# Four state groups of one channel half in a row, with B spread once per step, in the selective scan of a four-layer network

## The chip, the cores and the metric

The kernel runs on one core of a Trainium2 chip. The metric is the device time of one execution in microseconds (us). Seventeen runs of the kernel before have a median of 8440.55 us (8407.6 to 8468.6).

The engines are named as in the profile: PE (matrix products; PEld is its weight load), DVE (vector), ACT (activation), POOL (a second elementwise engine), SP (here it only issues DMAs).

## What is computed

The reference has four layers on a 4 x 96 x 64 x 64 tensor. Only layer 0 is touched. It runs two "mamba" blocks over each image, seen as a sequence of 4096 positions with 96 channels. A block, cut to what matters:

```python
xz = h @ in_w                                  # h: layer norm of seq
xs, z = jnp.split(xz, 2, axis=-1)              # 192 channels each
xc = silu(conv4(xs) + conv_b)                  # 4 taps along the sequence
dbl = xc @ xproj_w                             # dt (6), B (16), C (16)
delta = softplus(dt @ dt_w + dt_b)
dA = exp(delta[..., None] * A)                 # 192 channels x 16 states
dBx = delta[..., None] * Bm[:, :, None, :] * xc[..., None]
hstates = associative_scan(dA, dBx)            # h[t] = dA[t] h[t-1] + dBx[t]
y = einsum('bldn,bln->bld', hstates, Cm) + Dp * xc
seq = seq + (y * silu(z)) @ out_w
```

After the second block come a small product (`fus_w`) and a batch norm.

## The kernel before, in words

**Tiling.** A *unit* is one chunk of 512 positions of one image (4), one block i (2) and one chunk index (8): 64 units, in that order. The 192 channels are two halves of 96, the 16 states four groups nq of 4. One *step* handles one group of one half: 96 x 4 = 384 rows, held as three tiles of 128 partitions (32 channels x 4 states each). A unit has eight steps, numbered m = 0 to 7 here; a table `ORDER` says which group and half each is. The code calls a step v (over all units) and divides it into four quarters q = 0 to 3.

**A step.**
- `states_in` (L564): PE spreads the group's four rows of B from the tile `dbl` over 128 partitions, into the one PSUM bank `Bb`.
- `inputs` (L571, DVE): `bt = xR * Bb`, all three tiles at once. `xR` is delta*x of the half, each channel repeated for the 4 states.
- `decay` (L582, ACT): `a_ps = exp(A * dR)`, one of the three tiles, in one of three banks. `dR` is delta, repeated like `xR`.
- `states` (L598, DVE): the scan of one tile, three a step. It reads `a_ps` and writes `bt` in place.
- `outputs`: ACT copies the last column to `carry` (L606), then POOL multiplies `bt` by the broadcast rows of C (`Cb`, L607).
- `collect` (L621, L624, PE), two steps later: sums the 4 states of each channel into the bank `yp`; the first step of a half also adds `Dp * xc` (L621).

**Around the steps.** `output` (L635, ACT) copies a finished `yp`. `finish` is called in parts: POOL's `xc * sz` (L640); then PE's L644 (the residual) and L646 (the output product); then ACT's L648; and for i = 1 also PE's L654, then ACT's L656 with DVE's L657. `replicate` is six DMAs that make the `dR` and `xR` of a half from a DRAM tile `spread`.

**Preparation.** `prepare` computes all that a unit needs before its steps. It is a generator with 34 or 35 pieces between its yields. Counted from 0, those that matter here are: 0 L420, 3 L429 and the halo copy L434, 6 L440 (DVE), 7 L442, 8 and 9 the conv L450 (four matmuls a half, sixteen records in all), 11 and 12 L457, 13 to 15 the gate L460, L462, L464 on ACT and then POOL's L465, 18 L471 (`dbl`'s product), 20 L475 (its copy) with the DMA of the C rows, 21 L481, 23 and 24 L488/L489, 25 L491, 26 L494, 27 L497 (DVE), 28 L503 with POOL's L504 and PE's L507, 29 POOL's L509, 30 L516 with POOL's L517, 31 to 33 the second gate L522, L524, L527 and POOL's L528.

**What sets the order.** The schedule is manual: each engine gets its instructions in the order in which the loop at L676 to L708 emits them. At quarter 4m + q of unit u it first calls the pieces of the next units that are due. With PERIOD 32, piece k of unit u+1 is due at quarter k - AHEAD of unit u (negative: in the unit before). Then, in this order and each at its own quarter: a part of `finish`, `states_in` of the next step (q = 1), `output`, `collect` of the step two back (q = 3), the scan and the decay two ahead (q = 0, 1, 2), and at q = 3 `outputs` of this step and `inputs` of the next.

With AHEAD 14, the conv falls in step 6, L471 in step 1, L504 and L509 in step 3, L517 and L528 in step 4. L640 is issued at step 2, q = 2, and L644 with L646 at step 4, q = 1.

B is spread five times a unit: where two neighbouring steps have the same group, they use the same `Bb`.

**Buffers before.** `bt` four tiles, `Cb` six, `dR` and `xR` three each; PSUM banks: two `mm` (all of `prepare`'s and `finish`'s products), three `a_ps`, one `Bb`, two `yp`.

Of the kernel before, what the change touches and what calls it, by code (L numbers as in the profile page):

```python
# [10 lines left out]
F32 = mybir.dt.float32  # L11
# [4 lines left out]
PSUM = bass.MemoryType.PSUM  # L16
DRAM = bass.MemoryType.DRAM

B, C, H, W = 4, 96, 64, 64
# [320 lines left out]
def layer0(k, X):  # L340

    tc, nc, ins = k.tc, k.nc, k.ins
    T = NB
    NCH = L // T
    NQ, NG, PS = 4, 3, 4
    NT = 2 * NQ
    ORDER = ((0, 0), (0, 1), (1, 0), (1, 1), (2, 0), (3, 0), (3, 1), (2, 1))
    LAST = {hf: max(m for m, o in enumerate(ORDER) if o[1] == hf) for hf in range(2)}
    with ExitStack() as es:

        nc.scalar.preload_act_table_set("natural_log_exp_and_others")
# [9 lines left out]
        seln = k.load(wp, "c_seln", (128, NQ, 128))  # L361
# [24 lines left out]
        def pool(name, bufs, **kw):  # L386
            return scan.enter_context(tc.tile_pool(name=f"l0{name}", bufs=bufs, **kw))

        p1, p2, p3 = pool("p1", 1), pool("p2", 2), pool("p3", 3)
        bp, cp = pool("b", 4), pool("c", 6)  # L390
        dram = pool("dram", 3, space=DRAM)
        pm, pa = pool("pm", 2, space=PSUM), pool("pa", 3, space=PSUM)
        pb, py = pool("pb", 1, space=PSUM), pool("py", 2, space=PSUM)
        fbs = {}

        def mm():
# [19 lines left out]
        def prepare(b, i, ch, st, before):  # L416
# [25 lines left out]
            nc.scalar.activation(h[:, 3:], d, AF.Identity, bias=k.v(f"ln_b{i}"))  # L442
            yield

            xc = st["xc"] = p3.tile([C, 2, T], F32, name="xc")
            ps = []
            for hf in range(2):
                p = mm()
# [4 lines left out]
                ps.append(p)  # L453
                yield
            yield
            for hf, p in enumerate(ps):
                nc.scalar.activation(xc[:, hf], p[:C], AF.Identity, bias=k.v(f"conv_b{i}{hf}"))  # L457
                yield
# [17 lines left out]
            out = dram.tile([16, T], F32, name="out_states")  # L476
            nc.sync.dma_start(out, dbl[64:80])
            yield
            ps = [mm() for _ in range(2)]
# [42 lines left out]
            nc.scalar.activation(gate, sz, AF.Exp, scale=-1.0)  # L522
            yield
            nc.scalar.activation(gate, gate, AF.Ln, bias=k.one[:C])  # L524
            replicate(st, 0)
            yield
            nc.scalar.activation(gate, gate, AF.Exp, scale=-1.0)  # L527
            nc.gpsimd.tensor_mul(sz, sz, gate)  # L528
            yield
            st["Cb"] = [cp.tile([128, T], F32, name="Cb") for _ in range(NQ)]  # L530
            for nq, t in enumerate(st["Cb"]):
                nc.sync.dma_start(
                    t, out[PS * nq : PS * nq + PS].unsqueeze(0).to_broadcast([32, PS, T])
                )
            yield

        def replicate(st, hf):

            for n, name in enumerate(("dR", "xR")):
                t = st[name, hf] = p3.tile([128, NG, T], F32, name=name)  # L540
                for q in range(NG):
                    r = 96 * hf + 32 * q
                    nc.sync.dma_start(
                        t[:, q], st["spread"][n, r : r + 32].unsqueeze(1).to_broadcast([32, PS, T])
                    )

        units = [(b, i, ch) for b in range(B) for i in range(2) for ch in range(NCH)]
        V = NT * len(units)
        sts = [{} for _ in units]
        carries, bts, Bbs, dec, skips = {}, {}, {}, {}, {}  # L550

        def at(v):

            u, m = divmod(v, NT)
            return (sts[u], units[u], *ORDER[m])

        def states_in(v):

            st, _, nq, _ = at(v)
            if v and v % NT and ORDER[v % NT - 1][0] == nq:  # L560
                Bbs[v] = Bbs[v - 1]
                return
            Bb = Bbs[v] = pb.tile([128, T], F32, name="Bb")
            nc.tensor.matmul(Bb, seln[:, nq], st["dbl"], start=True, stop=True)  # L564

        def inputs(v):

            st, _, nq, hf = at(v)
            bt = bts[v] = bp.tile([128, NG, T], F32, name="bt")
            Bb = Bbs[v]  # L570
            nc.vector.tensor_mul(  # L571
                bt, st["xR", hf], Bb.unsqueeze(1).to_broadcast([128, NG, T])
            )

        def decay(n):

            v, q = divmod(n, NG)
            if v >= V:
                return
            st, (b, i, ch), nq, hf = at(v)  # L580
            dec[n] = pa.tile([128, T], F32, name="a_ps")
            nc.scalar.activation(  # L582
                dec[n], st["dR", hf][:, q], AF.Exp, scale=A[:, i, nq, hf, q : q + 1]
            )
# [17 lines left out]
        def outputs(v):  # L602

            st, _, nq, hf = at(v)
            bt = bts[v]
            nc.scalar.copy(carry_of(v), bt[:, :, T - 1])  # L606
            nc.gpsimd.tensor_mul(  # L607
                bt, bt, st["Cb"][nq].unsqueeze(1).to_broadcast([128, NG, T])
            )

        def collect(v):

            st, (b, i, ch), nq, hf = at(v)
            if nq == 0:
                yp = st["yp", hf] = py.tile([C, T], F32, name="yp")
                if ch == 0:
                    skips[hf] = p1.tile([C, C], F32, name=f"skip{hf}")
                    nc.vector.tensor_scalar(
                        skips[hf], k.ident[:C, :C], k.v(f"Dp{i}{hf}"), None, ALU.mult
                    )  # L620
                nc.tensor.matmul(yp, skips[hf], st["xc"][:, hf], start=True, stop=False)  # L621
            bt = bts.pop(v)
            for q in range(NG):
                nc.tensor.matmul(  # L624
                    st["yp", hf][32 * q : 32 * q + 32],
                    red,
                    bt[:, q],
                    start=False,
                    stop=v % NT == LAST[hf],
                )  # L630

        def output(u, hf):

            st, (b, i, ch) = sts[u], units[u]
            nc.scalar.copy(st["xc"][:, hf], st["yp", hf])  # L635
# [21 lines left out]
            nc.vector.bn_stats(stats[:, b, ch], xs)  # L657
            yield

        PERIOD, AHEAD = 4 * NT, 14  # L660

        with tc.manual_schedule():
            for _ in pooled(0):
                pass
            for _ in prepare(*units[0], sts[0], None):
                pass
            replicate(sts[0], 1)
            states_in(0)
            inputs(0)
            for n in range(2):  # L670
                decay(n)
            preps = [
                prepare(*units[u], sts[u], sts[u - 1]) if u else iter(()) for u in range(len(units))
            ]
            taken, task = [0] * len(units), iter(())
            for v in range(V + 7):  # L676
                u, m = divmod(v, NT)
                for q in range(4):
                    for w in range(u + 1, min(u + 3, len(units))):
                        while taken[w] <= 4 * v + q - PERIOD * (w - 1) + AHEAD:  # L680
# [12 lines left out]
                    if q == 2 and m == 2 and 0 < u <= len(units):  # L693
                        task = finish(u - 1)
                        next(task)
                    if q == 3 and 0 <= v - 2 < V:
                        collect(v - 2)
                    if v >= V:
                        continue
                    if q < NG:  # L700
                        states(NG * v + q)
                        decay(NG * v + q + 2)
                    if q == 3:
                        outputs(v)
# [1493 lines left out]
```

## Time and profile before

| | us |
|---|---|
| median of 17 runs | 8440.55 |
| the profiled execution | 8448.68 |
| its span, first to last instruction | 8446.9 |
| layer 0's steps: first L571, last L571 | 105.80, 3454.15 |

Busy in the stretch from 105 to 3460 (3355.0 us), with the granted clock of PE as a share of full speed:

| PE | PEld | DVE | ACT | POOL | PE clock |
|---|---|---|---|---|---|
| 2557.61 | 826.10 | 2873.04 | 2265.52 | 2637.20 | 0.83 |

How to read the lines that follow. A line of the timeline has the start, the duration, the engine, the line of the code, the operation, output <- inputs, the shapes and the number of instructions merged into the line; in brackets stands how long the engine had been idle and whom it waited for by the trace. "issue" there means a wait that the profile could not put down to anyone. A line of the groups has the count, then total busy us and the mean ns of one, then the engine's idle time just before. A line of the waits has the total us, how often, and the longest. An f32 matmul of the code shows as two records.

### The profile page before, as it was taken

The numbers are of one execution on the slowest core, as the hardware profiler recorded it, in microseconds if no ns is written. First come the engines' busy times: TensorE is split into PE (matmuls) and PEld (weight loads), VectorE is DVE, ScalarE is ACT, GpSimd is POOL, SyncE is SP. The second block draws the span as 40 slices with busy tenths as digits, with TensorE's granted clock in tenths as the row PEclk, the third lists the DMA queues.
The fourth block names the chain that finished last, engine by engine and source line by source line (L and its number), as shares of the span: only waits on it lengthen the run. The fifth ranks groups of instructions, "written<-read, shape, count | busy, mean of one in ns | idle before, by whom it ended". The sixth has DMA issues, their size and how long they took to land.

```text
span 8446.9 us, 76871 instructions
## 1 busy us (share of the span) xinstructions
PE 5981.6 (71%) x24218; PEld 2790.4 (33%) x24218; DVE 5719.6 (68%) x8127; ACT 3946.3 (47%) x7624; POOL 4696.2 (56%) x2915
## 2 busy tenths in 40 slices
PE   4777777777777777656688989897765656556553
PEld 1222222222222222422255555555442323333221
DVE  4888888888888888578865554545445555556555
ACT  4666666666666666333345555555521111111101
POOL 4877777778777877334444342424005555545553
PEclk8888888888888888777878888888877777767676
DMA  3322222222222222423210101010025444344443
GB/s 104 105 96 95 93 98 95 95 96 95 95 95 96 95 96 95 146 75 90 75 47 4 36 4 35 6 34 14 16 55 145 114 123 138 109 134 117 114 115 122
DMA packets 424413, 720.32 MB, mean 85 GB/s; under 512 B 188149, under 2 KB 190253, under 8 KB 419762
## 3 DMA queue, kind: packets, MB, share of 16 engines
q1 hardware_dynamic: 348710, 480.74, 18.4%
q0 software_dynamic: 73968, 227.47, 9.5%
q10 hardware_dynamic: 1328, 7.20, 0.2%
q8 instruction: 193, 3.16, 0.2%
q14 instruction: 214, 1.75, 0.1%
HBM read 567.04 MB, written 97.82 MB: 79 GB/s over the span
## 4 chain that ended last, share of the span: by engine, by line
PE 31%; DVE 18%; another core or an unknown queue 8%; ACT 7%; issue 7%; DMA 2%; POOL 2%; SPq 1%; DVEq 0%; ACTq 0%; POOLq 0%
PE sc_ps L1069 2%; DVE bt L598 2%; PE mm_ps L450 2%; PE pT_ps L1118 2%; DVE bt L571 2%; PE o_ps L1138 2%; DVE prod L2010 1%; PE yb_ps L1916 1%; DVE sm L2011 1%; PE yd_ps L2043 1%; PE Bb L564 1%; PE sT_ps L2031 1%; PE mm_ps L471 1%; PE m_ps L1527 1%
## 5 line engine op out<-in xcount | busy, mean ns | idle before, releaser
L607 POOL TENSOR_TENSOR bt<-bt,Cb 128x1536 f32<-128x1536 f32 x512 | 1763.4, 3444 | 678.2 <-issue 451.2
L598 DVE TENSOR_TENSOR_SCAN bt<-a_ps,carry,bt 128x512 f32<-128x512 f32 x1536 | 1865.1, 1265 | 58.2 <-ACT a_ps L582 11.0
L1993 POOL DMA_INDIRECT sm<-table,ix x1152 | 1097.2, 952 | 1300.4 <-DVE om L1970 494.7
L582 ACT ACTIVATE a_ps<-dR,w_l_A_log 128x512 f32<-128x512 f32 x1536 | 1053.2, 687 | 343.4 <-DVE bt L598 339.2
L571 DVE TENSOR_TENSOR bt<-xR,Bb 128x1536 f32<-128x1536 f32 x512 | 889.2, 1737 | 399.2 <-issue 189.8
L2031 PE MATMUL sT_ps<-ident,sd 128*128 128x128 f32 (+1 forms) x896 | 226.8, 376 | 716.8 <-ACT sT L2032 447.3
L564 PE MATMUL Bb<-dbl,w_c_seln 128*128 128x512 f32 x640 | 449.8, 792 | 380.1 <-DVE bt L571 380.1
L1106 POOL TENSOR_TENSOR p<-p,rs 128x392 f32<-128x392 f32 x384 | 312.0, 840 | 477.3 <-DVE rs L1104 417.1
L450 PE MATMUL mm_ps<-h,Wk 96*128 96x512 f32 x1024 | 567.3, 717 | 11.1 <-issue 6.8
L624 PE MATMUL yp<-bt,w_c_red 128*32 128x512 f32 x3072 | 560.3, 635 | 6.0 <-POOL bt L607 6.0
L471 PE MATMUL mm_ps<-xc,w_l_xp 96*128 96x512 f32 x256 | 235.6, 1076 | 290.9 <-POOL xc L465 290.9
L2031 PEld LDWEIGHTS sT_ps<-ident,sd 128*128 128x128 f32 (+1 forms) x896 | 133.9, 182 | 795.1 <-ACT sT L2032 474.3
L319 PE MATMUL bc_ps<-xs,w_l_bc 96*128 96x512 f32 x384 | 241.8, 763 | 215.3 <-DVE q L913 215.3
L1093 ACT ACTIVATE p<-p,rs 128x196 f32<-128x196 f32 x768 | 342.7, 449 | 82.6 <-DVE rs L1083 82.4
L2032 ACT COPY sT<-sT_ps 128x512 f32<-128x512 f32 (+1 forms) x256 | 122.0, 477 | 523.6 <-PE sT_ps L2031 266.4
L450 PEld LDWEIGHTS mm_ps<-h,Wk 96*128 96x128 f32 x1024 | 241.0, 238 | 365.2 <-issue 332.6
L2048 DVE SCALAR_TENSOR_TENSOR z<-yd_ps,vec,yb 96x512 f32<-96x512 f32 x32 | 23.9, 747 | 498.5 <-remote 286.5
L564 PEld LDWEIGHTS Bb<-dbl,w_c_seln 128*128 128x128 f32 x640 | 137.3, 242 | 652.2 <-DVE bt L571 493.2
L1929 ACT ACTIVATE go<-go_ps,w_l_go_b 18x512 f32<-18x512 f32 x32 | 21.7, 678 | 703.4 <-remote 524.3
L1916 PE MATMUL yb_ps<-X,w_l_base_w 96*128 96x504 f32 (+3 forms) x576 | 309.5, 702 | 0.3 <-ACT go L1930 0.3
L1126 DVE COPY pT<-pT_ps 98x512 f32<-98x512 f32 x256 | 176.0, 687 | 153.1 <-PE pT_ps L1118 145.6
L507 PE MATMUL mm_ps<-h,w_l_z_w 96*128 96x512 f32 x256 | 222.1, 1017 | 77.9 <-ACT w L503 77.9
(372 smaller groups left out, 13150.9 us busy)
## 6 DMA issues: line engine op xcount, KB each, us to landing
dR<-spread SPq DMA_DIRECT2D x384, 256.0 KB
xR<-spread SPq DMA_DIRECT2D x384, 256.0 KB
Cb<-out_states SPq DMA_DIRECT2D x256, 256.0 KB
spread<-w SPq DMA_DIRECT2D x128, 192.0 KB
spread<-dx SPq DMA_DIRECT2D x128, 192.0 KB
table<-xT SPq DMA_DIRECT2D x256, 96.0 KB
own<-vd SPq DMA_DIRECT2D x512, 36.8 KB
toep<-l_toep SPq DMA_DIRECT2D x12, 1536.0 KB
```

The source lines that it names most:

```text
L450: nc.tensor.matmul(p, Wk[:, i, t, hf], h[:, t : t + T], start=t == 0, stop=t == 3)
L471: nc.tensor.matmul(p, xp[:, i, hf], xc[:, hf], start=hf == 0, stop=hf == 1)
L564: nc.tensor.matmul(Bb, seln[:, nq], st["dbl"], start=True, stop=True)
L571: nc.vector.tensor_mul(bt, st["xR", hf], Bb.unsqueeze(1).to_broadcast([128, NG, T]))
L582: nc.scalar.activation(dec[n], st["dR", hf][:, q], AF.Exp, scale=A[:, i, nq, hf, q : q + 1])
L598: nc.vector.tensor_tensor_scan(t, dec.pop(n), t, carry_of(v)[:, q : q + 1], ALU.mult, ALU.add)
L607: nc.gpsimd.tensor_mul(bt, bt, st["Cb"][nq].unsqueeze(1).to_broadcast([128, NG, T]))
L624: nc.tensor.matmul(st["yp", hf][32 * q : 32 * q + 32], red, bt[:, q], start=False, stop=v % NT == LAST[hf],)
L1093: nc.scalar.activation(ps[n][:, h, i], ps[n][:, h, i], AF.Exp, scale=-1.0, bias=rs[n][:, 0, h, i : i + 1], accum_out=rs[n][:, 1, h, i : i ...
L1916: nc.tensor.matmul(dv[:, r0:r1, c0:c1], w_[:, t], av[b][:ch, 8 * n + r0 + dy : 8 * n + r1 + dy, c0 + dx : c1 + dx], start=t == 4, stop=t == 8,
L1993: nc.gpsimd.indirect_dma_start(sm[u][:, t].rearrange("p q c -> p (q c)"), None, samples[m // NN % 2], bass.IndirectOffsetOnAxis(ap=ix[m][: ...
L2031: nc.tensor.transpose(p[: e - 128 * q, q - q0], sf[:, 128 * q : e], k.ident)
```

## The change

1. The order of a unit's steps becomes: groups 0 to 3 of half 0 (steps 0 to 3), then groups 0 to 3 of half 1 (steps 4 to 7). The tables `ORDER` and `LAST` go.
2. `states_in` spreads B in every step, eight times a unit; no `Bb` serves two steps.
3. Buffers: `bt` six tiles, `dR` and `xR` two each; three `mm` banks, one `yp` bank.
4. AHEAD is 24 instead of 14, so every piece of `prepare` is emitted ten quarters earlier. The `xc` tile is taken after the conv's products instead of before them.
5. The replicating DMAs leave `prepare`: half 0 of the next unit is issued at step 3, q = 1, half 1 at step 7, q = 1. The broadcasts of C become a function, two groups each at steps 6 and 7, q = 3.
6. `output` is called at step 6 for half 0 and at step 2 of the next unit for half 1 (before: steps 1 and 2 of the next unit). The parts of `finish` after the first are called at (3,1), (3,3), (4,1), (4,3) instead of (4,1), (5,0), (5,1), (5,3).

```diff
-    ORDER = ((0, 0), (0, 1), (1, 0), (1, 1), (2, 0), (3, 0), (3, 1), (2, 1))
-    LAST = {hf: max(m for m, o in enumerate(ORDER) if o[1] == hf) for hf in range(2)}
...
-        bp, cp = pool("b", 4), pool("c", 6)
+        bp, cp = pool("b", 6), pool("c", 6)
...
-        pm, pa = pool("pm", 2, space=PSUM), pool("pa", 3, space=PSUM)
-        pb, py = pool("pb", 1, space=PSUM), pool("py", 2, space=PSUM)
+        pm, pa = pool("pm", 3, space=PSUM), pool("pa", 3, space=PSUM)
+        pb, py = pool("pb", 1, space=PSUM), pool("py", 1, space=PSUM)
...
             nc.scalar.activation(gate, gate, AF.Ln, bias=k.one[:C])
-            replicate(st, 0)
             yield
             nc.scalar.activation(gate, gate, AF.Exp, scale=-1.0)
             nc.gpsimd.tensor_mul(sz, sz, gate)
             yield
-            st["Cb"] = [cp.tile([128, T], F32, name="Cb") for _ in range(NQ)]
-            for nq, t in enumerate(st["Cb"]):
-                nc.sync.dma_start(
-                    t, out[PS * nq : PS * nq + PS].unsqueeze(0).to_broadcast([32, PS, T])
-                )
-            yield
...
-                t = st[name, hf] = p3.tile([128, NG, T], F32, name=name)
+                t = st[name, hf] = p2.tile([128, NG, T], F32, name=name)
...
+        def broadcast(st, nq):
+
+            t = st["Cb", nq] = cp.tile([128, T], F32, name="Cb")
+            src = st["out"][PS * nq : PS * nq + PS]
+            nc.sync.dma_start(t, src.unsqueeze(0).to_broadcast([32, PS, T]))
...
-            return (sts[u], units[u], *ORDER[m])
+            return (sts[u], units[u], m % NQ, m // NQ)
...
-            if v and v % NT and ORDER[v % NT - 1][0] == nq:
-                Bbs[v] = Bbs[v - 1]
-                return
-            Bb = Bbs[v] = pb.tile([128, T], F32, name="Bb")
-            nc.tensor.matmul(Bb, seln[:, nq], st["dbl"], start=True, stop=True)
+            Bbs[v] = pb.tile([128, T], F32, name="Bb")
+            nc.tensor.matmul(Bbs[v], seln[:, nq], st["dbl"], start=True, stop=True)
...
-        PERIOD, AHEAD = 4 * NT, 14
+        PERIOD, AHEAD = 4 * NT, 24
...
-            replicate(sts[0], 1)
+            for hf in range(2):
+                replicate(sts[0], hf)
+            for nq in range(NQ):
+                broadcast(sts[0], nq)
...
-                    if (m, q) in ((4, 1), (5, 0), (5, 1), (5, 3)):
+                    if (m, q) in ((3, 1), (3, 3), (4, 1), (4, 3)):
                         next(task, None)
...
+                    if q == 1 and m == 6 and u < len(units):
+                        output(u, 0)
+                    if q == 1 and m == 2 and 0 < u <= len(units):
+                        output(u - 1, 1)
+                    if u + 1 < len(units):
+                        if q == 1 and m in (3, 7):
+                            replicate(sts[u + 1], m // NQ)
+                        if q == 3 and m in (6, 7):
+                            for nq in (2 * m - 12, 2 * m - 11):
+                                broadcast(sts[u + 1], nq)
                     if q == 1 and v + 1 < V:
                         states_in(v + 1)
-                    if q == 1 and m in (1, 2) and 0 < u <= len(units):
-                        output(u - 1, m - 1)
...
-                        if m == LAST[0] and u + 1 < len(units):
-                            replicate(sts[u + 1], 1)
```

More of the change, by code (lines that the diff above doesn't have):

```diff
@@ L443, in prepare @@
             yield
-            xc = st["xc"] = p3.tile([C, 2, T], F32, name="xc")
             ps = []
@@ L455, in prepare @@
             yield
+            xc = st["xc"] = p3.tile([C, 2, T], F32, name="xc")
             for hf, p in enumerate(ps):
@@ L475, in prepare @@
             nc.scalar.copy(dbl, p)
-            out = dram.tile([16, T], F32, name="out_states")
+            out = st["out"] = dram.tile([16, T], F32, name="out_states")
             nc.sync.dma_start(out, dbl[64:80])
@@ L569, in inputs @@
             bt = bts[v] = bp.tile([128, NG, T], F32, name="bt")
-            Bb = Bbs[v]
+            Bb = Bbs.pop(v)
             nc.vector.tensor_mul(
@@ L607, in outputs @@
             nc.gpsimd.tensor_mul(
-                bt, bt, st["Cb"][nq].unsqueeze(1).to_broadcast([128, NG, T])
+                bt, bt, st["Cb", nq].unsqueeze(1).to_broadcast([128, NG, T])
             )
@@ L628, in collect @@
                     start=False,
-                    stop=v % NT == LAST[hf],
+                    stop=nq == NQ - 1,
                 )
```

## The prediction

> **How to count.** A unit is one 512-column chunk; its eight steps s0..s7 have four quarters q0..q3. Piece k of `prepare` (the code between two yields, from 0) runs at quarter k minus AHEAD of the unit before its own. All times are us.
>
> **What bounds it now.** I read the busy shares first, then the groups of the layer-0 stretch, the waits of that stretch, and then one unit in order of time. Layer 0's step loop runs from the first L571 at 105.80 to the last at 3454.15: 511 steps, 6.553 each, 52.42 a unit. The groups and the waits:
>
> ```profile
> L607 POOL TENSOR_TENSOR bt<-bt,Cb 128x1536 f32<-128x1536 f32 x512 | 1763.4, 3444 | 678.2 <-issue 451.2
> L598 DVE TENSOR_TENSOR_SCAN bt<-a_ps,carry,bt 128x512 f32<-128x512 f32 x1536 | 1865.1, 1265 | 58.2 <-ACT a_ps L582 11.0
> L571 DVE TENSOR_TENSOR bt<-xR,Bb 128x1536 f32<-128x1536 f32 x512 | 889.2, 1737 | 399.2 <-issue 189.8
> ```
> ```profile
> DVE bt L571 <- issue: 189.8, 59, 4.4
> DVE bt L571 <- PE Bb L564: 188.7, 97, 4.0
> ```
>
> DVE does the scans and sets the pace: a step without a wait takes 5.41 (L571 at 2009.47 and 2014.88). Eight steps, with 1.17 for the L497 pair and 0.44 for L440, make 44.9. The unit shown next (i = 0) took 51.51, so some 6.6 is waiting, all before L571, at two places:
>
> ```profile
> 2031.63 1.12 PE L644 MATMUL mm_ps<-X,ident 96*128 96x512 f32 x2
> ...
> 2032.60 1.88 PE L646 MATMUL mm_ps<-xc,w_l_out_w 96*128 96x512 f32 x4
> ...
> 2034.31 1.02 PE L564 MATMUL Bb<-dbl,w_c_seln 128*128 128x512 f32 x2
> ...
> 2035.44 1.75 DVE L571 TENSOR_TENSOR bt<-xR,Bb 128x1536 f32<-128x1536 f32 x1 [3.11 <-PE Bb L564]
> ...
> 2044.50 8.93 PE L450 MATMUL mm_ps<-h,Wk 96*128 96x512 f32 x16
> ...
> 2053.36 1.06 PE L624 MATMUL yp<-bt,w_c_red 128*32 128x512 f32 x6
> ...
> 2054.34 1.13 PE L564 MATMUL Bb<-dbl,w_c_seln 128*128 128x512 f32 x2
> ...
> 2055.57 1.75 DVE L571 TENSOR_TENSOR bt<-xR,Bb 128x1536 f32<-128x1536 f32 x1 [3.40 <-issue]
> ```
>
> Both times L571 starts 0.1 after L564 ended. L564 (the B spread) is short, but PE's matmuls run in code order, and it stands behind the output product L646 (s4) or behind the conv L450 (s6). The second wait, which the page puts down to "issue", is thus also for Bb and not for a bt buffer.
>
> **What costs nothing.** Six bt tiles: no wait for a bt buffer is seen above. Three more B spreads a unit: 0.86 of PE each (L564 2034.31 to L420 2035.17); each may start when L571 has freed the one Bb bank (1.75 into a step) and needs 1.0 to 2.1, so it ends 1.5 before DVE wants it, unless something stands ahead of it; that is priced below. With the cover gone it costs its own 1.0 to 2.1. Two replication tiles: the half-0 DMAs are issued at s3q1, after the last reads of that half, and read first from s7q1, four steps (21.6) later; six issues took 4.0 here and the first xR was used 6.2 after its issue. Half 1 and the C broadcasts have at least one step more than that queue needs; SP's waits hold no other engine's work. One yp bank: the copy L635 is two quarters ahead of the L621 that needs the bank. Three mm banks: each bank's reader (L503, L516, L425, L440, L648) stands quarters before the next writer. If an ACT copy were late there, PE would lose its 0.6.
>
> **What the earlier preparation does.** AHEAD 24 moves every piece by ten quarters against the scan. On POOL, L504 (piece 28), L509 and L517 fall in s1q0..q2, L528 in s2q1, and L640 stays at s2q2. POOL's order from s0 on becomes L607(s0), L504, L509, L517, L607(s1), L528, L640. `finish`'s second part (L644, L646) moves from s4q1 to s3q1, where it stands on PE ahead of the B spread for s4. So that spread now waits for L640; behind it on PE stand a collect and the conv. DVE waits for the spread, ACT's L457 for the conv. POOL's starts in this trace:
>
> ```profile
> 1028.30 3.44 POOL L607 TENSOR_TENSOR bt<-bt,Cb 128x1536 f32<-128x1536 f32 x1 [0.86 <-POOL xc L640]
> 1031.69 2.36 POOL L504 TENSOR_TENSOR dx<-dx,e 96x1024 f32<-96x1024 f32 x1
> 1034.12 2.35 POOL L509 TENSOR_TENSOR w<-w,dx 96x1024 f32<-96x1024 f32 x1
> 1036.43 3.45 POOL L607 TENSOR_TENSOR bt<-bt,Cb 128x1536 f32<-128x1536 f32 x1
> 1039.85 2.35 POOL L517 TENSOR_TENSOR dx<-w,xc 96x1024 f32<-96x1024 f32 x1
> 1042.16 2.37 POOL L528 TENSOR_TENSOR sz<-sz,gate 96x1024 f32<-96x1024 f32 x1
> 1044.50 3.42 POOL L607 TENSOR_TENSOR bt<-bt,Cb 128x1536 f32<-128x1536 f32 x1
> ```
>
> From one start to the next: 3.4 for L607, 2.43 for L504, 2.3 for the others. Two L607, L504 and four others make 18.6 from L607(s0)'s start to L640's end. Let 0 be the end of s0's scans. DVE wants s4's B spread at 18.0 (L497 1.17, three steps, L440 0.6). The sum of a unit with i = 0:
>
> - L607(s0) starts at 1.15: ACT must first copy the carry, and in s0 it now also has L488/L489, L491 and L494. Nearest row: 2021.70, 1.33 after the scans ended, with the same pieces about; without them 0.3. I count ACT's work through s0 (5.85 against DVE's 5.41) and get 1.15.
> - L640 ends at 19.75.
> - L646 and the B spread then take 2.73 with PE at speed (2032.60 to 2035.33) or 4.53 after a long pause. The pause: L644 has what it needs by about 14.5 and is done by 15.6, an estimate from the rows of L429, L621 and L624, so 4.2. The nearest row is L471, which paused 4.42; it and the spread behind it took 4.53 (2010.24 to 2014.77). I take 4.53. s4's L571 starts at 24.4, a wait of 6.4.
>
> ```profile
> 2010.24 3.30 PE L471 MATMUL mm_ps<-xc,w_l_xp 96*128 96x512 f32 x4 [4.42 <-POOL xc L465]
> ...
> 2013.33 1.44 PE L564 MATMUL Bb<-dbl,w_c_seln 128*128 128x512 f32 x2
> ...
> 2024.70 3.78 PE L507 MATMUL mm_ps<-h,w_l_z_w 96*128 96x512 f32 x4 [1.50 <-ACT w L503]
> ```
>
> - The conv (pieces 8 and 9) falls in s4q0 and s4q1, ahead of the spread for s5: collect 0.86, sixteen passes of 0.43 (1.71 for L646's four) or 6.9 at speed, 8.86 as in the unit shown (2044.50 to 2053.36); right behind other work I take 7.0. With the spread's 1.02 and the hand-over, s5's L571 starts 8.83 after the spread of s4 ended, where DVE wants it after 5.5: a second wait of 3.3.
> - Three steps, 16.2. Then the spread for the next s0 needs `dbl`, now copied (L475) only at s7q0: gate, L465 (2.35), L471 (3.3), L475 (0.6), L481 (1.9) and the spread end 16.0 to 17.4 after s5 began, against 16.2. I take 0.4. Then s0 itself, 5.45.
>
> Sum: 1.15 + 18.6 + 0.06 + 4.53 + 8.83 + 16.2 + 0.4 + 5.45 = 55.2. For i = 1, L654, L656 and L657 stand ahead of s5's L571: +1.3 (1.1 for L654, 0.7 each for the others, less the spread they replace). Mean 55.9, 3.45 over 52.42; 63 units have a following unit: +217. At the start, 25 instead of 15 pieces of unit 1 go ahead of the third decay of step 0: gate Exp 1.0, L465 2.4, L471 3.8, L475 0.6, L481's first half 2.1 and four of L488/L489 2.5, with six hand-overs of 0.1, make +13. Together +230 on the profiled run's 8448.7 (span 8446.9): 8679. The median of the runs lies 8 lower: **8671**.
>
> [...] L507 paused only 1.50, after a thin stretch, and its four passes still took 3.78, twice L646's 1.88; the granted clock over the loop is 0.83. [...]
>
> **Rivals.**
> - *PE stays fast* (0.20): L646 and the spread take 2.73. 1.8 less in 63 units: 8558. For it: spreads that paused 2.58 ran in 1.12. Against it: L471 never ran at speed.
> - *More goes cold or late* (0.15): the conv takes 8.86 as now (+117) and the `dbl` chain ends 1.3 late instead of 0.4 (+57): up to 8845.
> - *Faster* (0.10): the POOL chain is hidden. It decides at L640's end: if that came by 15.2 (18.0 less 2.8) instead of 19.75, s4 would not wait, and a unit would be 18.0 + 8.7 + 22.05 = 48.8, or 50.1 for i = 1: 3.0 less than now, 8440 - 189 + 13 = 8264. For it: POOL is idle a fifth of the loop (2637.2 busy of 3355). Against it: L607(s0) cannot start before s0's scans end, and 18.6 of POOL follows.
> - *It cancels* (0.05): L640 about 2 earlier than I count and PE fast; within 0.2% of 8440, which is about what a measurement of this kernel can tell from no change.
>
> **Numbers.** My case has 0.50, 8610 to 8730. With every low end together (0.3 for the carry, PE fast, no wait at s0) a unit still takes 52.1 and 53.4, and the time is near 8475: if the order of work is as I read it, it is not faster. Range 8530 to 8800: it leaves out the last two rivals and the top of the second. Faster 0.10, same 0.05, slower 0.85.
>
> **What would show it.** L640 as what PE's L646 waits for, some 4 long, once a unit; L571 waiting for Bb twice a unit, about 6 at s4 and 3 at s5, none at s6 or s7; at most 1 at s0; a unit of 55 to 57. It is wrong if L646 doesn't wait for L640, or if the conv's spread is in time.

## The result, and the profile after

The changed kernel takes 8721.28 us (8 runs, 8701.2 to 8733.6) against 8432.6 for the kernel before (46 runs); the ratio is 1.0337, 95% interval 1.0323 to 1.0352. The profiled execution took 8725.08, its span is 8723.3, 276.4 longer than before. All of that lies in layer 0's step loop: from its first to its last `bt = xR * Bb` it takes 3633.30 (102.42 to 3735.72) where it took 3348.35, 285 more. The code has lost some lines, so L571 is now L564, the scan L591, the B spread L557, the decay L575, POOL's product L600, the carry L599, the skip tile (L618 before) L611, L617 collects, L633 is POOL's `xc * sz`, L637 and L639 are the residual and the output product, L650 the statistics, L447 the conv, L469, L473 and L479 the chain of `dbl`.

The groups of the page, and the waits of DVE in the loop (total, times, longest):

```profile
L600 POOL TENSOR_TENSOR bt<-bt,Cb 128x1536 f32<-128x1536 f32 x512 | 1756.3, 3440 | 666.3 <-ACT carry L599 476.9
...
L564 DVE TENSOR_TENSOR bt<-xR,Bb 128x1536 f32<-128x1536 f32 x512 | 889.5, 1737 | 509.7 <-PE Bb L557 354.7
```
```profile
DVE bt L564 <- PE Bb L557: 354.7, 94, 6.1
DVE bt L564 <- issue: 139.1, 60, 7.4
DVE stats L650 <- ACT X L649: 136.6, 32, 16.2
```

The engines' own work is what it was: 512 products of 3.44 each, and 1536 scans (L591) that sum to 1865.7 where they summed to 1865.1. What grew is the idle time before L564, from 399 to 510, and the wait of the statistics, behind which the same instruction stands when i = 1: 39.7 in 31 waits before, 120.4 in 31 waits now (the longest of the line above, 16.2, comes behind the last L564). Over units 1 to 62 the mean distance from the L564 (L571) of one step to that of the next is, worked out from the starts in the traces:

| | s0 | s1 | s2 | s3 | s4 | s5 | s6 | s7 | unit |
|---|---|---|---|---|---|---|---|---|---|
| before, i = 0 | 5.41 | 5.72 | 5.48 | 6.59 | 8.36 | 5.61 | 5.85 | 8.85 | 51.88 |
| after, i = 0 | 6.59 | 5.32 | 5.86 | 10.18 | 9.04 | 5.40 | 5.86 | 7.46 | 55.72 |
| after, i = 1 | 6.60 | 5.32 | 6.02 | 10.09 | 9.94 | 5.33 | 6.02 | 8.05 | 57.37 |

A wait lengthens the column of the step before it. So DVE waits ahead of s4, of s5 and of the next s0. One unit with i = 0, in order of time; its s0 is the L564 at 2120.09:

```profile
2109.00 3.78 PE L469 MATMUL mm_ps<-xc,w_l_xp 96*128 96x512 f32 x4 [0.40 <-POOL xc L463]
2112.58 1.91 PE L614 MATMUL yp<-xc,skip 96*96 96x512 f32 x2
2114.42 1.93 PE L617 MATMUL yp<-bt,w_c_red 128*32 128x512 f32 x6
2116.28 2.86 PE L479 MATMUL mm_ps<-dbl,w_l_dt_w 128*128 128x512 f32 x4
2118.98 1.02 PE L557 MATMUL Bb<-dbl,w_c_seln 128*128 128x512 f32 x2
2120.09 1.75 DVE L564 TENSOR_TENSOR bt<-xR,Bb 128x1536 f32<-128x1536 f32 x1 [3.87 <-issue]
...
2126.04 3.44 POOL L600 TENSOR_TENSOR bt<-bt,Cb 128x1536 f32<-128x1536 f32 x1 [2.85 <-ACT carry L599]
...
2142.35 2.35 POOL L633 TENSOR_TENSOR xc<-xc,sz 96x1024 f32<-96x1024 f32 x1
2144.75 1.98 PE L639 MATMUL mm_ps<-xc,w_l_out_w 96*128 96x512 f32 x4 [1.21 <-POOL xc L633]
2146.57 1.02 PE L557 MATMUL Bb<-dbl,w_c_seln 128*128 128x512 f32 x2
2147.64 1.75 DVE L564 TENSOR_TENSOR bt<-xR,Bb 128x1536 f32<-128x1536 f32 x1 [4.13 <-PE Bb L557]
2148.52 7.14 PE L447 MATMUL mm_ps<-h,Wk 96*128 96x512 f32 x16
2155.49 1.02 PE L557 MATMUL Bb<-dbl,w_c_seln 128*128 128x512 f32 x2
2156.55 1.75 DVE L564 TENSOR_TENSOR bt<-xR,Bb 128x1536 f32<-128x1536 f32 x1 [3.42 <-PE Bb L557]
```

All three times L564 starts 0.04 to 0.09 after a spread that stood behind something else on PE: behind L639 (which waited for L633) at s4, behind the sixteen records of the conv at s5, behind L469, a collect and L479 at s0. The third is one that the page calls "issue". The unit is typical: in 45 of the units 1 to 62, L639 started within 0.1 of the end of L633. In the other 17, the seven first chunks among them, PE itself was still behind.

There is a second loss. In the first of a block's eight chunks the steps s2 and s6 take 10.3 instead of 5.4, and there DVE's small skip tile is what takes long (its median is 5.02, against 0.376 before, sixteen times):

```profile
146.29 5.82 DVE L611 TENSOR_SCALAR skip<-ident,vec 96x96 f32<-96x96 f32 x1
146.32 3.42 POOL L600 TENSOR_TENSOR bt<-bt,Cb 128x1536 f32<-128x1536 f32 x1
149.70 2.34 POOL L525 TENSOR_TENSOR sz<-sz,gate 96x1024 f32<-96x1024 f32 x1
...
152.02 1.74 DVE L564 TENSOR_TENSOR bt<-xR,Bb 128x1536 f32<-128x1536 f32 x1
```

L611 ends when two POOL products in a row have ended, and the next L564 stands behind it. Before, it fell into a gap of POOL's or less than 0.9 before the end of a product, and never took more than 0.85: 0.24 at 135.86, for example, with POOL idle and its next product at 137.21.

### The profile page after: what moved, and what is told of

It reads as the page before. It is cut to its first block, busy times and chain, and to the rows that moved or that the text cites. A ratio compares the mean times of both kernels' runs of the same rounds, so it can differ in the third digit from the quotient of the medians.

```text
span 8723.3 us, 77362 instructions
## 1 busy us (share of the span) xinstructions
PE 6227.2 (71%) x24602; PEld 2781.4 (32%) x24602; DVE 5796.2 (66%) x8127; ACT 3925.9 (45%) x7624; POOL 4689.7 (54%) x2915
## 4 chain that ended last, share of the span: by engine, by line
PE 26%; DVE 15%; another core or an unknown queue 8%; issue 6%; ACT 5%; POOL 3%; DMA 2%; SPq 1%; DVEq 0%; ACTq 0%; POOLq 0%
PE sc_ps L1071 2%; PE pT_ps L1120 2%; PE o_ps L1140 2%; DVE prod L2012 1%; DVE bt L591 1%; DVE sm L2013 1%; PE yb_ps L1918 1%; PE bc_ps L319 1%; PE m_ps L1529 1%; SPq L1877 1%; PE yd_ps L2045 1%; PE mm_ps L447 1%; DVE bt L564 1%; PE p_ps L1163 1%
## 5 line engine op out<-in xcount | busy, mean ns | idle before, releaser
L600 POOL TENSOR_TENSOR bt<-bt,Cb 128x1536 f32<-128x1536 f32 x512 | 1756.3, 3440 | 666.3 <-ACT carry L599 476.9
L591 DVE TENSOR_TENSOR_SCAN bt<-a_ps,carry,bt 128x512 f32<-128x512 f32 x1536 | 1865.7, 1266 | 73.2 <-ACT a_ps L575 24.8
L575 ACT ACTIVATE a_ps<-dR,w_l_A_log 128x512 f32<-128x512 f32 x1536 | 1049.1, 686 | 731.8 <-DVE bt L591 725.4
L564 DVE TENSOR_TENSOR bt<-xR,Bb 128x1536 f32<-128x1536 f32 x512 | 889.5, 1737 | 509.7 <-PE Bb L557 354.7
L557 PE MATMUL Bb<-dbl,w_c_seln 128*128 128x512 f32 x1024 | 643.3, 714 | 427.8 <-DVE bt L564 421.2
L617 PE MATMUL yp<-bt,w_c_red 128*32 128x512 f32 x3072 | 646.5, 712 | 6.1 <-POOL bt L600 6.1
L447 PE MATMUL mm_ps<-h,Wk 96*128 96x512 f32 x1024 | 462.2, 604 | 6.1 <-issue 3.1
L557 PEld LDWEIGHTS Bb<-dbl,w_c_seln 128*128 128x128 f32 x1024 | 187.4, 210 | 816.6 <-DVE bt L564 708.5
L463 POOL TENSOR_TENSOR xc<-xc,gate 96x1024 f32<-96x1024 f32 x64 | 150.3, 2349 | 362.7 <-issue 304.9
L447 PEld LDWEIGHTS mm_ps<-h,Wk 96*128 96x128 f32 x1024 | 190.7, 191 | 280.0 <-issue 235.6
L2012 DVE TENSOR_TENSOR prod<-sm,cws 128x960 f32<-128x960 f32 (+1 forms) x256 | 270.8, 1058 | 6.7
```

The lines of the kernel that those rows point to most:

```text
L447: nc.tensor.matmul(p, Wk[:, i, t, hf], h[:, t : t + T], start=t == 0, stop=t == 3)
L557: nc.tensor.matmul(Bbs[v], seln[:, nq], st["dbl"], start=True, stop=True)
L564: nc.vector.tensor_mul(bt, st["xR", hf], Bb.unsqueeze(1).to_broadcast([128, NG, T]))
L575: nc.scalar.activation(dec[n], st["dR", hf][:, q], AF.Exp, scale=A[:, i, nq, hf, q : q + 1])
L591: nc.vector.tensor_tensor_scan(t, dec.pop(n), t, carry_of(v)[:, q : q + 1], ALU.mult, ALU.add)
L600: nc.gpsimd.tensor_mul(bt, bt, st["Cb", nq].unsqueeze(1).to_broadcast([128, NG, T]))
```

## The experiments

The theory was that of the prediction: the ten quarters by which the preparation comes earlier put L639, the conv and the chain of `dbl` ahead of spreads that DVE needs. PE took its work in code order in the traces of both kernels: its records of layer 0's steps and of all that is called around them (6480 before, 6864 after) stand in the order of the calls. The rivals: the new order of the steps itself costs (more spreads, six bt tiles, fewer banks), or POOL's product chain paces the unit whatever PE does. Some runs were on a chip on which the rest of the network is faster (the kernel before takes 7861 there) while the loop is the same (3629.87 and 3633.30 for the changed kernel with four bt tiles there and with six here); so ratios to the kernel before on the same chip, and loop times, are compared. For each run in the table, the loop's difference from the kernel before agrees to 15 us with the difference of the medians on its own chip. "Loop" is always first to last L564 of the profiled execution; expected times of the 8400 scale are read as ratios there.

| run | ratio [95%] | loop | mean unit |
|---|---|---|---|
| before | 1 | 3348.4 | 52.37 |
| after | 1.0337 [1.0323, 1.0352] | 3633.3 | 56.55 |
| x1 spread ahead of `finish` | 1.0329 [1.0308, 1.0351] | 3621.4 | 56.36 |
| x2 spread first of all | 1.0278 [1.0239, 1.0318] | 3598.8 | 56.06 |
| x3 gate after L633 | 1.0233 [1.0210, 1.0256] | 3537.2 | 55.01 |
| x4 before, no shared spread | 0.9896 [0.9877, 0.9916] | 3273.7 | 51.18 |
| x5 after, AHEAD 14 | 0.9788 [0.9769, 0.9806] | 3197.1 | 49.92 |
| x6 after, four bt tiles | 1.0352 [1.0332, 1.0372] | 3629.9 | 56.49 |
| x8 s0's spread early | 1.0234 [1.0216, 1.0252] | 3528.1 | 54.94 |
| x9 x5, conv in halves, AHEAD 15 | 0.9797 [0.9771, 0.9823] | 3179.1 | 49.69 |
| x10 before, more PE work | 0.9926 [0.9905, 0.9947] | 3286.2 | 51.39 |
| x11 after, conv in halves | 1.0180 [1.0162, 1.0198] | 3493.2 | 54.30 |
| x12 x5, late statistics | 0.9782 [0.9761, 0.9802] | 3155.9 | 49.23 |
| x13 after, skip tile on ACT | 1.0275 [1.0252, 1.0299] | 3551.1 | 55.40 |

**x1: the spread stands ahead of `finish`'s part.** The call moves up within its quarter.

```diff
+                    if q == 1 and v + 1 < V:
+                        states_in(v + 1)
...
-                    if q == 1 and v + 1 < V:
-                        states_in(v + 1)
```

> The changed kernel (8721), with one swap: in its quarter, the B spread of the next step is emitted ahead of the part of finish, so at step 3 it no longer stands behind the output product (L639) and its wait for L633 on POOL. Theory (one PE queue, the waits at s4 and s5 are one backlog): the wait at s4 (mean 3.9) goes, but the conv still stands behind L639, so the spread for s5 comes some 11 after s4 began and the wait there grows from 3.1 to about 6.4 (i = 0); for i = 1 the batch-norm statistics come as late as before. Net 0.3 to 1.0 a unit less: 8650 to 8710. Rival (each wait has its own price): 3.9 less in 63 units, 8476.

The wait at s4 is nearly gone (s3 to s4 takes 6.79 instead of 10.18 for i = 0, 6.74 instead of 10.09 for i = 1), and s4 to s5 grew from 9.04 to 11.87 and from 9.94 to 13.38. In the unit that answers to the one above:

```profile
2144.59 7.14 PE L447 MATMUL mm_ps<-h,Wk 96*128 96x512 f32 x16
...
2152.63 1.75 DVE L564 TENSOR_TENSOR bt<-xR,Bb 128x1536 f32<-128x1536 f32 x1 [6.34 <-PE Bb L557]
```

The conv, still behind L639, starts 4.06 after s4's L564 (2140.53) instead of 0.88, so the wait is handed on to s5, most of it for i = 0 and all of it for i = 1: a wait taken from one spread is worth nothing while the next one stands behind a longer block.

**x2: the spread is the first thing of its quarter,** ahead of the preparation's pieces too (the same two lines, put higher).

> The changed kernel, with the B spread emitted first in its quarter, ahead of the pieces of prepare too: at step 3 ahead of L639, at step 4 between the two conv halves, at step 7 ahead of L479. Theory (the three waits are PE's order): s4 about 0; s5 about 3 for i = 0, where half the conv still stands ahead, and unchanged for i = 1, where the statistics wait for L647 behind the whole conv; s0 2.3 down to about 1 since 2.0 to 2.9 of L479 no longer stand ahead. Mean 3 to 4 less a unit: 8460 to 8540. Rival (what costs is the spread itself, eight a unit instead of five): no change, 8721. Rival (each wait has its own price): 8 less a unit, 8220.

A miss: 1.003 to 1.012 of the kernel before was expected, it is 1.028, and the loop lost 35. The conv runs over two quarters, and with i = 1 its second half with L647 still stands ahead of the statistics (13.52 from s4 to s5). With i = 0, `dbl` is late in another way:

```profile
2139.28 3.78 PE L469 MATMUL mm_ps<-xc,w_l_xp 96*128 96x512 f32 x4 [2.58 <-POOL xc L463]
...
2143.10 0.58 ACT L473 COPY dbl<-mm_ps 128x512 f32<-128x512 f32 x1 [3.61 <-PE mm_ps L469]
...
2144.31 1.28 DVE L591 TENSOR_TENSOR_SCAN bt<-a_ps,carry,bt 128x512 f32<-128x512 f32 x1 [0.85 <-ACT a_ps L575]
```

ACT's records too stand in the order of the calls in the traces of both kernels (3880 in each). Here its copy L473 waits 3.61 for L469, whose four passes took 3.78, the decays that come behind the copy start at 2143.58, and the scan waits 0.85 for one of them. The spreads were freed and ACT's queue took their place.

**x3: the gate's second half goes behind L633.** Two empty pieces ahead of the last two of the gate.

```diff
+            yield
+            yield
             nc.scalar.activation(gate, gate, AF.Exp, scale=-1.0)
             nc.gpsimd.tensor_mul(sz, sz, gate)
```

> The changed kernel, with two empty pieces in prepare ahead of the second gate's last part (L524, L525), so that POOL's L633 runs ahead of L525 and ends 2.35 earlier. Theory (POOL's chain sets s4's wait, with PE's own backlog 1.2 behind it in the trace): L639 gains 1.2, not 2.35; 1.2 less in 63 units: 8645. If PE's backlog were no bound: 8573. Rival (POOL's chain does not set it): 8721.

The wait at s4 fell by 1.47 to 2.55 (means of units 1 to 62), not by the 2.35 of the product that no longer stands ahead of L633; the loop lost 96. Outside the first chunks L633 ends 2.30 earlier (22.34 after s0's L564 instead of 24.64), but L639 starts only 1.54 earlier (23.19 instead of 24.73). POOL's chain does set s4, but PE's own backlog (below) is close behind it.

**x4: the kernel before with a spread in every step.** This is the change's second edit alone.

```diff
-            if v and v % NT and ORDER[v % NT - 1][0] == nq:
-                Bbs[v] = Bbs[v - 1]
-                return
```

> The kernel before (8433), with B spread in every step, eight times a unit instead of five, and nothing else of the change. Theory (a spread is hidden unless something stands ahead of it on PE): within 20 of 8433. Rival (the spread itself costs 0.86 to 1.1 each): three more in 64 units, 8600 to 8645.

Faster by 1.04%, where the theory had no change and the rival a loss. The gain sits in one column: s4 to s5 takes 6.89 instead of 8.36 (i = 0). The granted clock of PE from 200 to 3200 rose from 0.83 to 0.89, and the four passes of L507, which stand ahead of L644, L646 and s5's spread, took 3.78 in the row that the prediction shows. Here, in one of the units, behind the same pause, they took half of that:

```profile
2028.24 1.99 PE L507 MATMUL mm_ps<-h,w_l_z_w 96*128 96x512 f32 x4 [1.50 <-ACT w L503]
```

Not every unit gains: the four passes took under 2.5 in 23 of the units 1 to 62, where it was 7 before. For i = 0, s4 to s5 takes 5.66 in the units where they were fast and 8.05 where they were not, which ties the gain to them.

**x10: more work for PE, and nothing else.** To tell the clock from any other effect of the spreads, the kernel before gets matmuls with a zero weight in three collects of each unit; they add zero to `yp`.

```diff
+            if v % NT in (0, 3, 6):
+                for q in range(NG):
+                    nc.tensor.matmul(
+                        st["yp", hf][32 * q : 32 * q + 32],
+                        mean[:, C:],
+                        bt[:C, q],
+                        start=False,
+                        stop=False,
+                    )
```

> The kernel before, B shared as before, but in the collects of steps 0, 3 and 6 PE also multiplies the same bt by a block of zeros, which adds nothing to yp: as many passes more as three B spreads a unit, and nothing waits for them. It asks why a spread in every step made the kernel before faster (x4, 0.990 of before; its step loop 3274 against 3348). Theory (PE's granted clock: more work between its pauses keeps it up, so L507, L471 and the conv run faster): part of that gain, a loop of 3275 to 3325 and 0.990 to 0.998 of before, with a granted clock above 0.83 in the loop and L507's four passes nearer 2 than 3.8. Rival (the bank is freed a step earlier when no spread is shared): no gain, 1.000 to 1.005, clock as before.

Faster by 0.74%, with the clock at 0.87 and the gain in the same column (6.69). L507 in the kernel before and in this one (least, median and most ns of one record):

```profile
L507 PE MATMUL mm_ps<-h,w_l_z_w x256: 590/1061/1222, 89.4 to 3391.8; 96*128 96x512 f32 x128
```
```profile
L507 PE MATMUL mm_ps<-h,w_l_z_w x256: 590/942/1222, 86.6 to 3326.1; 96*128 96x512 f32 x128
```

Useless work on PE made the kernel faster. In the kernel before, 4676 of the 6433 PE records from 90 to 3460 took 0.57 to 0.62 and 1009 took 1.00 to 1.10 (worked out from the trace); L507, whose median record there is one of the slow ones, stands ahead of what DVE waits for, and its median fell from 1061 to 942 ns. As in x4, only a part of the units gains: the four passes took under 2.5 in 20 of 62 units.

**x5: AHEAD 14, all else as changed.**

```diff
-        PERIOD, AHEAD = 4 * NT, 24
+        PERIOD, AHEAD = 4 * NT, 14
...
-                        if q == 1 and m in (3, 7):
-                            replicate(sts[u + 1], m // NQ)
+                        if (m, q) in ((4, 3), (7, 1)):
+                            replicate(sts[u + 1], m // 7)
```

> The changed kernel (8721) with AHEAD 14 as before, and half 0's replication at step 4, quarter 3, where its source is ready; the new order of the steps, eight spreads, the buffers and the places of finish stay. Theory (the earlier preparation is what costs: it puts POOL's five products ahead of L633, the conv ahead of s5's spread, and dbl's product just ahead of s0's): the waits at s4 and s5 go, the conv stands ahead of s0's spread as in the kernel before (2.7 to 3.7): about 49.3 a unit, 7 less than now, and the long start goes: 8200 to 8330, below both kernels. Rival (the order of the steps and the spread per step cost): 8650 to 8721.

436 less in the loop than the changed kernel and 151 less than the kernel before. L639 hardly waits for L633 any more, and PE stays fast (clock 0.92):

```profile
2030.19 1.99 PE L639 MATMUL mm_ps<-xc,w_l_out_w 96*128 96x512 f32 x4 [0.31 <-POOL xc L633]
```

So AHEAD is what costs, and the rest of the change is a gain that it hides. That rest is the new order of the steps, the eight spreads, the buffers and the earlier calls of `finish` and `output` together; of these only the spreads were run alone, in the old order (x4, 1.04%).

**x6: four bt tiles instead of six** (`pool("b", 4)`).

> The changed kernel with four bt tiles instead of six. Theory (no engine waits for a bt tile): 8721, within 20. Rival (the two more tiles hide a wait for POOL's late products, so without them the time rises): 8760 or more.

The loop is the changed kernel's to 3.4: the two extra tiles neither cost nor bring anything.

**x8: the spread for s0 goes out before the late work.** At step 7 the spread comes first in its quarter, and the collect of s4 moves two quarters back.

```diff
+                    if q == 1 and v + 1 < V and m == 7:
+                        states_in(v + 1)
...
-                    if q == 1 and v + 1 < V:
+                    if q == 1 and v + 1 < V and m < 7:
                         states_in(v + 1)
...
-                    if q == 3 and 0 <= v - 2 < V:
+                    if q == 3 and 0 <= v - 2 < V and m != 6:
                         collect(v - 2)
+                    if q == 1 and 0 <= v - 3 < V and m == 7:
+                        collect(v - 3)
```

> The changed kernel with PE's order at the end of a unit altered: the collect of step 4 moves from step 6 to step 7, and the spread for the next s0 is emitted first in step 7's quarter 1, so after dbl's copy (L473) it stands ahead of L614, L617 and L479. Theory (s0's wait is these three on a slow PE): the wait at s0 (mean 2.3) goes, and of that about 1 comes back before L495, since the dt chain on ACT is no earlier against the scan: 8560 to 8660. Rival (s0 waits for the dbl chain itself, L463 to L473): within 20 of 8721.

The wait at s0 is gone (s7 to s0 takes 5.58 and 6.05 instead of 7.46 and 8.05), and a part comes back at s4 (11.12 instead of 10.18). Outside the first chunks POOL's first product starts 6.48 after s0's L564 instead of 5.99, and L639 was slow (over 2.5) in 17 of 55 units instead of 2:

```profile
2137.44 3.58 PE L639 MATMUL mm_ps<-xc,w_l_out_w 96*128 96x512 f32 x4 [1.54 <-POOL xc L633]
...
2142.02 1.75 DVE L564 TENSOR_TENSOR bt<-xR,Bb 128x1536 f32<-128x1536 f32 x1 [6.16 <-PE Bb L557]
```

The edit has a second effect. The collect that moves is the one that makes half 1's skip tile in a first chunk, and in its new place L611 takes 1.94 to 2.01 instead of 5.0. Eight times 3.0 is 24 of the 105 that the loop lost.

**x11: the conv's halves a step apart,** with AHEAD 27: the first half falls in step 3, ahead of L639, the second in step 4.

```diff
+                if hf == 0:
+                    yield
+                    xc = st["xc"] = p3.tile([C, 2, T], F32, name="xc")
+                    nc.scalar.activation(
+                        xc[:, 0], p[:C], AF.Identity, bias=k.v(f"conv_b{i}0")
+                    )
+                    yield
+                    yield
+            yield
+            yield
+            nc.scalar.activation(xc[:, 1], p[:C], AF.Identity, bias=k.v(f"conv_b{i}1"))
+            yield
...
-        PERIOD, AHEAD = 4 * NT, 24
+        PERIOD, AHEAD = 4 * NT, 27
```

> The changed kernel with the two conv halves four quarters apart: half 0 at step 3 quarter 0's neighbour (3, q 1), half 1 at step 4, quarter 1 as before; all later pieces stay where they are. Theory (s5's wait is the length of the conv ahead of its spread): the wait at s5 (i = 0: 3.1; i = 1: as a later L647) goes, s4's stays near 3.9, since PE waits there for L633 anyhow: 2.5 to 3 less a unit, 8530 to 8570. Rival (the conv only moves ahead of s4's spread and the wait with it): within 30 of 8721.

s4 to s5 fell from 9.04 and 9.94 to 5.61 and 6.62, about to DVE's own time; s2 grew from 5.86 to 8.07 in return, so of some 3.4 a unit 2.25 are left. AHEAD 27 brings the pieces ahead of the conv three quarters forward too: DVE's L438 (L440 in the kernel before) moves from s3 into s2. It takes 0.74 there and DVE waits 1.48 ahead of it, means outside the first chunks, while s3 gets shorter (8.75 instead of 10.18 for i = 0). The loop lost 140; the ratio of 1.018 is a little short of the gain expected (1.011 to 1.016).

**x12: x5 with the statistics two steps later** (the last part of `finish` at (5, 3) instead of (4, 3)).

> x5 (the changed kernel with AHEAD 14 and the later replication), with the last part of finish, ACT's L649 and DVE's statistics L650, four quarters later, at step 5, quarter 3. Theory (for i = 1 the scan waits in step 4 for L649, behind PE's L647, beyond the statistics' own 0.7: 7.39 from s4 to s5 against 5.65 for i = 0): about 1.2 less in 32 units, a loop of 3150 to 3170 against 3197, 0.972 to 0.977 of the kernel before. Rival (the wait moves along): 0.978 to 0.980.

The loop lost 41, which is the sum that the theory had, but not where it had it. For i = 1, s4 to s5 fell from 7.39 to 5.38, and s5 to s6 grew from 5.48 to 7.13: most of the wait moved along, as in the rival. The units with i = 0, most of which the edit leaves as they were, lost as much (48.73 to 48.05) as those with i = 1 (51.12 to 50.42). The profiled executions also lie apart, x5's 27 above the median of its runs and x12's 22 below its own, and the ratio (0.9782 against 0.9788, the intervals overlap) can't tell the two kernels apart. So no gain is shown.

**x9: x5 with the spread first and the conv's halves apart,** AHEAD 15.

> The changed kernel with what the runs so far point to: AHEAD 15 and the later replication as in x5, the B spread emitted first in its quarter, and the two conv halves four quarters apart (half 0 at step 6, quarter 1, half 1 at step 7, quarter 1, each behind that quarter's spread). Theory (what is left of x5's waits is the conv ahead of s0's spread, 2.5 for i = 0 and 3.2 for i = 1): the wait at s0 falls to 0.5 or less and nothing else grows; a unit of 47.0 to 48.0 against x5's 49.9, 0.955 to 0.966 of the kernel before. Rival (the pieces of prepare, one quarter later and with the gate behind, hold ACT and so the decays): 0.975 or more.

A miss, and the rival was right: s7 to s0 fell from 8.37 to 5.70, but s0, s2 and s5 grew from 5.41, 5.47 and 5.57 to 6.88, 6.61 and 6.21, where a scan (L597 in this kernel) now waits for a decay (L581). Ahead of that decay, which started at 2001.79, stands ACT's L461 (2000.05), which waited 3.76 for the conv's second half:

```profile
2002.49 1.28 DVE L597 TENSOR_TENSOR_SCAN bt<-a_ps,carry,bt 128x512 f32<-128x512 f32 x1 [1.57 <-ACT a_ps L581]
```

**x13: the skip tile on ACT.**

```diff
-                    nc.vector.tensor_scalar(
-                        skips[hf], k.ident[:C, :C], k.v(f"Dp{i}{hf}"), None, ALU.mult
-                    )
+                    nc.scalar.activation(
+                        skips[hf], k.ident[:C, :C], AF.Identity, scale=k.v(f"Dp{i}{hf}")
+                    )
```

> The changed kernel with L611, the 96x96 tile of the skip term, computed by ACT instead of by DVE (as an activation with a scale). In the changed kernel DVE's L611 takes 5.02 in the median, sixteen times, and each one ends where POOL's back-to-back products end; in the kernel before it took 0.376. Theory (DVE is held up behind POOL, and the steps pay for it): 4.6 x 16 = 74 go where DVE is what sets the pace (the eight at half 1), and less where the wait for B at step 4 follows in any case (the eight at half 0's end are ahead of it): the loop falls by 30 to 74, to 3560 to 3603, a ratio of 1.025 to 1.030. The first chunk of a block shows steps 2 and 6 at 5.4 to 5.8 instead of 10.3. Rival (the long record is only its waiting for work that DVE would have waited for in any case): step 2 or 6 keeps its 10, the loop stays within 10 of 3633, a ratio of 1.033 to 1.035.

The loop lost 82, a little over the 74 of the sum, and the first chunks' units fell from 64.0 and 62.8 to 55.4 and 55.2; their s2 and s6 take 5.38. L611 at the place shown above, with the L564 that it held up now at 147.33:

```profile
147.80 0.37 ACT L611 ACTIVATE skip<-ident,vec 96x96 f32<-96x96 f32 x1
```

So the long record is a real loss, not a wait that DVE would have had anyway.

## Why the prediction was right, and where it was off

The direction, the mechanism and the two main places were right. The size was 46 short (276 of span against 230). That it came so near owes something to luck, since the terms were off in both directions: over 63 units the wait at s4 was counted some 150 too high (6.4 against a mean of 4.02) and the wait at s0 some 108 too low (0.4 against 2.12), and the skip tile's 82 were not counted at all. Point by point:

- *POOL's chain.* 18.6 from L607(s0) to L640's end was predicted; 18.66 was measured (2126.04 to 2144.70). It started 0.46 after s0's scans, not 1.15.
- *The wait at s4.* 6.4 was predicted, 4.13 measured (mean 4.02). The step that was mis-sized is "L644 has what it needs by about 14.5 and is done by 15.6 ... so 4.2": the residual ran 16.8 to 18.0 after s0's scans, because PE was itself behind (L427 waited 2.96 for ACT's L424, and a skip product of 1.92 and a collect of 1.54 followed). L639 thus paused 1.21 and ran at speed; it and the spread took 2.84, not 4.53. The sign "some 4 long" thus failed. The rival "PE stays fast" had this one term right. x3 shows the same backlog from the other side, as 1.47 of 2.35. In x8 L639 paused 1.54 and took 3.58, in the changed kernel it paused 1.21 and took 1.98, but L507 took 3.78 or 1.99 behind the same pause of 1.50: the rows have no clean bound at which a pause makes PE slow.
- *The conv's wait at s5.* 8.83 from the end of s4's spread to s5's L564 was predicted, 8.96 measured (2147.59 to 2156.55); wait 3.3 and 3.42. x11 takes it away.
- *The wait at s0.* 0.4 was predicted, 3.87 measured in the unit shown; the mean is 2.12, about the same for both i. The sign "at most 1 at s0" thus failed. The sum for "gate, L465 (2.35), L471 (3.3), L475 (0.6), L481 (1.9) and the spread" left out the collect of s4, which stands on PE between L471 and L481: L614 and L617, 1.91 and 1.93 on a slow PE; and L481's successor took 2.86, not 1.9. x8 takes this wait away.
- *i = 1.* 1.3 more was predicted; outside the first chunks it is 56.58 against 54.84, 1.74.
- *The skip tile.* Not in the sum at all. With it on ACT (x13) the loop is 3551, 203 above before, where the sum had 230; the other 82 are this one instruction. So without it the terms above, one too large, one too small, would have been 27 too high together.
- *The start.* 13 was predicted, 26 measured (unit 0: 88.80 against 62.64); with the skip tile on ACT it is 14.5.
- *What costs nothing.* Right for the six bt tiles (x6). For the spreads it was right as an upper bound only: with PE's granted clock at 0.89 instead of 0.83 they gained 1.04% in the kernel before (x4).
- *The cause.* That the ten quarters do it, and not the new order, was argued; x5 shows it. What the prediction did not price is that the rest of the change alone would win 2.1%. Taking away one wait at a time (x3, x8, x11) gave 96, 105 and 140, and x13 gave 82; these were not run together, so that they add up is not shown. Their sum of 423 is near x5's 436, but x8 and x13 share some 24 of it, the skip tile of half 1.

What stays open: which part of the rest of the change brings x5's gain, and at what load PE turns slow. The best versions run (x5, x9, x12) are level at about 2% under the kernel before.

## What to carry to other kernels

Where an engine takes its work in code order, list for each piece that is moved what is queued behind it, through all engines: here the product waiting for POOL, the long conv and a collect each held a one-microsecond spread that DVE needed, and moving one of them handed a part of the wait to the next (x8, x11), or nearly all of it (x1). Getting ready earlier is no gain by itself; each engine's backlog at the new place decides, and small one-time instructions must be placed as well. When a change that bundles several edits loses, run each alone: here one number (AHEAD) hid a gain of 2%.

## What the runs showed of the hardware

**DVE's TENSOR_SCALAR ended with POOL's products.** In the changed kernel the 96x96 tile (L611) took 4.96 to 5.82, sixteen times, beside two POOL products in a row, and ended 0.06 to 0.07 after the second; it was not let in between the two (L525 began at 149.70, as L600 ended). In the kernel before it took 0.24 with POOL idle; the other fifteen took 0.24 to 0.85, began less than 0.9 before the end of a product and ended 0.06 to 0.10 after it. In x8 half 1's tile took 1.94 to 2.01 in its new place, and on ACT (x13) both halves' took 0.36 to 0.37. What holds DVE up there is not seen in any record.

**PE took 3.78 or 1.99 for the same work.** These are L507's four passes behind the same pause of 1.50, in the kernel before and in x4. The granted clock from 200 to 3200 was 0.83 before, 0.87 with useless matmuls added, 0.89 with three more spreads a unit, 0.84 in the changed kernel, 0.92 in x5. The useless matmuls paid for themselves: 0.74%.
